# Second mixture of experts: weighted rows added into the output by indirect DMA instead of being stored, gathered and summed

## Chip, cores and metric

The kernel runs on one core of a Trainium2 chip. The metric is device time in microseconds (us) for one execution. The kernel before has a median of 2408.45 us over three runs (2401.93, 2408.45 and 2413.18).

## The reference, cut to what matters

The input is x, 4096 tokens of 256 features, and a 4096 x 4096 adjacency matrix. Two layers follow each other. Layer 0 is a graph convolution with a Mamba scan and then a mixture of eight experts; layer 1 is a graph convolution and then a mixture of six experts with three matrices each. The change touches only the last mixture:

```
rh = relu(features @ router_w1 + router_b1)          # features = layernorm(x)
expert_logits = softmax(rh @ router_w2 + router_b2)
top_w, top_i = top_k(expert_logits, 2)               # two experts of six per token
routing_weights = softmax(top_w)
h1 = relu(features @ expert_w1 + expert_b1)
h2 = relu(h1 @ expert_w2 + expert_b2)
expert_out = h2 @ expert_w3 + expert_b3
x = x + sum over the two chosen experts of routing_weights * expert_out
```

So each output row is the token's row of x (called x3 in the kernel) plus two weighted expert rows.

## The kernel before, in words

Tokens are handled in eight chunks of 512 (four groups of 128 partitions). The last mixture is split in two dispatches: `d1a` has chunks 0 to 5, `d1b` chunks 6 and 7 (lines 1452 to 1456). A `Dispatch` (L163) routes tokens to experts. Its normalised tokens go to a DRAM table `xd` (L473); a `Part` builds index tables in `tables` (L293): `src`, the row of `xd` behind each slot, and `dst`, the row of `ys` in which the slot's result belongs. An expert tile is 256 slots of one expert, in two halves j = 0 and 1 of 128. There are 27 tiles for `d1a` and 11 for `d1b` (list `few`, L1636), 38 in all, run in that order.

One tile, `tile_of` (L528): two indirect gathers on GpSimd's queue bring its rows into `xk` (`fetch`, L427 to L433, four buffers); SyncE's queue brings three matrices `wk` of 256 KB and the bias row `bk` (L535, L538); TensorE transposes (L542), VectorE copies to `xkT` (L546), TensorE runs two layers (L521) that ScalarE evacuates (L525). `finish` (L498) then multiplies by the third matrix into `ps_y` (L502), VectorE adds the bias into `yk` (L510, three buffers; in the last tile by halves, L507), and `put` (L435) sends each half by an indirect DMA from GpSimd's queue to its rows of `ys` (L437). The finish of tile k-1 is written between the first and second layers of tile k. The framework's scheduler orders each engine's list when the kernel is built; the lists run in order. Puts go to distinct rows; one put waits only for the put four before it.

The sums stand behind the tiles. `combine` (L559) reads a chunk's two result rows per token from `ys` into `yg` (L570), after the dispatch's last puts, and two VectorE operations per 128 tokens (L577) multiply by the routing weights `wv` and add x3. `to_out` (L1618) stores the chunk `oc` to the output (L1626). The six chunks of `d1a` are summed while the tiles of `d1b` run (function `also`, L1664); the two of `d1b` after the last tile, their loads shared by SyncE's and ScalarE's queues. At the very end a flag is computed; VectorE's copy `flagi` (L1689) waits for the last put, every engine loads it (L1690), and a branch (L1694) skips a rarely needed second computation.

Routing of chunks 0 to 6 is done inside the loop of the second graph convolution (`route_of`, called at step j2 of each chunk; 16 steps per chunk, TensorE line L1555); chunk 7 is routed by `routing` while the first tiles run.

Of the kernel before, what the change touches and what calls it, by code (L numbers as in the profile page):

```python
# [30 lines left out]
def kernel(ctx: ExitStack, tc: tile.TileContext, out: bass.AP, **a):  # L31
# [131 lines left out]
    class Dispatch:  # L163
# [4 lines left out]
        def __init__(self, pool, E, name, batches, c0=0):  # L168

            self.E, self.pool, self.name, self.T, self.c0 = E, pool, name, batches, c0  # L170
            self.t0 = [sum(batches[:b]) for b in range(len(batches))]
# [6 lines left out]
            self.xd = dram.tile([NT * P, D], F32, name=f"{name}_xd")  # L178

            self.S = 1 << (NT // TPC - 1).bit_length()  # L180
            self.ys = dram.tile([2 * self.S * CW + self.K * TR, D], F32, name=f"{name}_ys")
            self.count = pool.tile([P, 1, E], F32, name=f"{name}_count")
            self.start()
            self.sent = []
# [93 lines left out]
    class Part:  # L278
# [3 lines left out]
        def __init__(self, dp, name, F, c0=0, full=False, xd=None):  # L282
            self.dp, self.name, self.F, self.c0, self.full = dp, name, F, c0, full
            self.C = F * TR // P
            self.xd = dp.xd if xd is None else xd
            pool = dp.pool
            self.src = pool.tile([P, self.C], I32, name=f"{name}_src")
            self.dst = pool.tile([P, self.C], I32, name=f"{name}_dst")
            self.exps = pool.tile([P, F], I32, name=f"{name}_exps")
            self.tiles = pool.tile([1, 1], F32, name=f"{name}_tiles")  # L290
            self.used = pool.tile([P, E0], F32, name=f"{name}_used") if full else None

        def tables(self, ps, tp, biases, NG, other=None, hots=None):  # L293
# [108 lines left out]

            nc.vector.tensor_scalar(grp, grp, TPC - 1, None, ALU.bitwise_and)
# [31 lines left out]
        def put(self, k, yk, j):  # L435
            dp, c = self.dp, k * (TR // P) + j
            s_ = nc.gpsimd.indirect_dma_start(  # L437
                out=dp.ys[:, :],
                out_offset=bass.IndirectOffsetOnAxis(ap=self.dst[:, c:c + 1], axis=0),
                in_=yk[:, j, :], in_offset=None,  # L440
            )

            for o in dp.sent[-3:]:
                tc.declare_no_dep(s_.ins, o.ins, reason="distinct rows")
            if len(dp.sent) > 3:
                after(s_, dp.sent[-4])
            dp.sent.append(s_)
# [9 lines left out]
    class Route:  # L457
# [9 lines left out]
        def prepare(self, b):  # L467
# [5 lines left out]
            nc.sync.dma_start(tokens(dp.xd, b), xn)  # L473
# [17 lines left out]

    def expert_tiles(jobs, psum, pool, weights, bias_out, layers, kb_out, also=None):
# [4 lines left out]
        def finish(dp, k, w, bk, hT, parts=1):  # L497
            ps = ps_o.tile([P, 2, D], F32, name="ps_y")  # L498
            yk = pool.tile([P, 2, D], F32, name="yk", bufs=3)
            for j in range(2):  # L500
# [5 lines left out]
                if parts == 2:  # L506
                    nc.vector.tensor_tensor(yk[:, j, :], ps[:, j, :], bk, ALU.add)  # L507
                    dp.put(k, yk, j)
            if parts == 1:
# [18 lines left out]
        def tile_of(dp, k, prev):  # L528
            e = dp.expert(k)
            xk = pool.tile([P, 2, D], F32, name="xk", bufs=4)  # L530
# [15 lines left out]
            nc.vector.tensor_copy(hT, ps)  # L546
            for n, (mb, func) in enumerate(layers):
# [3 lines left out]
            return dp, k, ws[-1], bk, hT  # L551
# [817 lines left out]
    with ExitStack() as s2:  # L1369
        with ExitStack() as st:  # L1370
# [83 lines left out]
            Dispatch(keep1, E1, "d1a", [TPC] * SPLIT),  # L1454
            Dispatch(keep1, E1, "d1b", [TPC] * (NC - SPLIT), SPLIT),
# [123 lines left out]

        early = [route1(d, wk, ps_m, ("m", "m", "m"), 4) for d in dp1]  # L1580

        def route_of(c):
# [9 lines left out]
            def step(j2):  # L1592
                if j2 == 2:
# [22 lines left out]
    stores = []  # L1616

    def to_out(d, b, pool, parts=1, queue=nc.sync, bufs=3, later=False):  # L1618


        c, T = d.c0 + b, TPC // parts
        o = pool.tile([P, TPC, D], F32, name="oc")
        sent = []

        def store(part):
            sent.append(nc.sync.dma_start(tokens(out, c)[:, part, :], o[:, part, :]))  # L1626
            return sent

        rows = x3[:, c * TPC:(c + 1) * TPC, :]
        for i, _ in enumerate(combine(d, pool, b, rows, o, parts, queue, bufs)):  # L1630
            if not later:
                store(slice(i * T, (i + 1) * T))
        return (lambda: store(slice(0, TPC))) if later else sent
# [3 lines left out]
    with ExitStack() as s4:  # L1637
# [10 lines left out]
        def routing():  # L1648
# [3 lines left out]
            yield  # L1652
            yield from part1s[1].tables(
# [4 lines left out]
        ready, held, op = list(range(SPLIT)), [], []  # L1658

        def also(n):  # L1660
            if n == few[0]:
                assert next(pieces, None) is None
                sr.close()
                op.append(s4.enter_context(tc.tile_pool(name="out1", bufs=2, reuse_waits="tile")))  # L1664
            elif n < few[0]:
                if n > 2:
                    next(pieces, None)
            else:

                while held:  # L1670
                    stores.append(held.pop()())
                if (n - few[0]) % 3 != 0 and ready:
                    held.append(to_out(dp1[0], ready.pop(0), op[0], bufs=4, later=True))

        tiles1([(d, k) for d, f in zip(part1s, few) for k in range(f)], psums, tp, also)
        assert not ready and not held

        for b in range(NC - SPLIT):
            stores.append(to_out(dp1[1], b, op[0], 2 * (b + 1), nc.scalar, 4))
# [14 lines left out]
    with tc.If(again > 0):  # L1694
# [57 lines left out]
        with ExitStack() as s3:  # L1752
# [21 lines left out]
            for c in range(NC):  # L1774
                for new in to_out(d, c, op):
                    for old in stores[c]:
                        after(new, old)
# [67 lines left out]
```

## Time and profile before

| what | value |
|---|---|
| median of the runs | 2408.45 us |
| the profiled execution's own time | 2390.19 us |
| span of its profile | 2388.4 us |
| mean granted TensorE clock | 0.968 |
| TensorE matmul busy | 2232.7 us (93%) |
| VectorE, ScalarE, GpSimd busy | 1647.1, 1197.2, 1149.4 us |
| DMA on SP's and ACT's hardware queues | 54.5 and 0.2% of 16 engines' span |
| DMA on GpSimd's software queue | 19.4% |
| tiles of the last mixture, first put to last put | 2133.6 to 2369.6 us |

The span is smaller than the execution's own time by 1.8 us. A group line names the source line, the engine, the operation, output and inputs, the count, busy time, the mean duration, and the idle time just before with its releaser. DMA-issuing instructions are not counted as busy on the page, but the timeline shows them with their duration. The time to landing of a DMA counts from the start of the issuing instruction.

### The profile page before, as it was taken

To read this page: it belongs to the slowest core of one execution; us is meant where nothing else is said; L and a number is where in the kernel's file an instruction comes from. 1 tells how busy PE (TensorE), PEld (TensorE's weight loads), DVE (VectorE), ACT (ScalarE), POOL (GpSimd) and SP (SyncE) were. 2 spreads that over 40 slices of the span, in tenths; PEclk is the share of its full clock that TensorE was granted. 3 is DMA by queue.
4 is the path that set the end of the run, shared out by engine and by line. 5 is a ranking of instruction groups with operands and counts; after the bars stand their busy time and mean duration, and the time that the engine had idled before them with its cause. 6 is when DMAs were issued, how large, how long until landed. Compare 5 with 4: busy or idle time off the path is not lost. (4 is left out here: it accounts for less than half of the span.)

```text
span 2388.4 us, 28122 instructions
## 1 busy us (share of the span) xinstructions
PE 2232.7 (93%) x9010; PEld 1624.8 (68%) x9010; DVE 1647.1 (69%) x2455; ACT 1197.2 (50%) x2056; POOL 1149.4 (48%) x836
## 2 busy tenths in 40 slices
PE   8999999999999999897997999889999999999985
PEld 7665665656566655554666888667788888878874
DVE  2069999999999999999986411182666666734233
ACT  4255666575556657476753322144555555633321
POOL 1057787777877777777644555310000000046652
PEclk9999999999999999998998999989999999999998
DMA  7278899999999999998848877541444444457787
GB/s 239 82 232 229 237 276 239 270 247 270 248 252 268 234 273 237 276 266 234 280 143 276 283 235 231 164 165 61 132 142 149 144 147 142 149 167 224 245 279 238
DMA packets 295136, 513.69 MB, mean 215 GB/s; under 512 B 25648, under 2 KB 160944, under 8 KB 294080
## 3 DMA queue, kind: packets, MB, share of 16 engines
q1 hardware_dynamic: 246400, 411.07, 54.5%
q0 software_dynamic: 47424, 99.12, 19.4%
q8 instruction: 75, 1.23, 0.2%
q10 hardware_dynamic: 1152, 1.57, 0.2%
q14 instruction: 85, 0.70, 0.1%
HBM read 406.03 MB, written 44.83 MB: 189 GB/s over the span
## 5 line engine op out<-in xcount | busy, mean ns | idle before, releaser
L1146 POOL TENSOR_TENSOR db<-du,bb 128x1024 f32<-128x1024 f32 x256 | 607.0, 2371 | 314.5 <-DVE hc L1179 77.4
L1169 DVE TENSOR_TENSOR_SCAN db<-da,state,db 128x512 f32<-128x512 f32 x512 | 627.4, 1266 | 22.2 <-ACT da L1162 19.9
L675 PE MATMUL pt<-at,gn 128*128 128x256 f32 x2048 | 478.0, 386 | 14.6 <-ACT gn L87 9.3
L675 PEld LDWEIGHTS pt<-at,gn 128*128 128x128 f32 x2048 | 396.1, 194 | 135.5 <-issue 63.3
L1162 ACT ACTIVATE da<-dt,negA 128x512 f32<-128x512 f32 x512 | 346.0, 688 | 245.7 <-DVE db L1169 236.1
L1555 PE MATMUL pf<-gn,f 128*128 128x256 f32 x2048 | 452.6, 380 | 0.5 <-ACT gn L1528 0.5
L1555 PEld LDWEIGHTS pf<-gn,f 128*128 128x128 f32 x2048 | 386.5, 190 | 57.8 <-issue 6.4
L1179 DVE TENSOR_TENSOR hc<-db,cb 128x1024 f32<-128x1024 f32 x256 | 328.0, 1281 | 18.3 <-issue 0.4
L1196 PE MATMUL psy<-hc,ident 128*128 128x512 f32 x560 | 291.1, 614 | 2.4 <-DMA hc<-hc 1.4
L81 POOL TENSOR_TENSOR ln_rs<-ln_rs,mhalf 128x4 f32<-128x4 f32 (+1 forms) x25 | 32.8, 1314 | 511.0 <-DVE ln_rs L80 510.5
L510 DVE TENSOR_TENSOR yk<-ps_y,bk 128x512 f32<-128x512 f32 x71 | 49.1, 691 | 291.0 <-PE ps_y L502 262.8
L1544 ACT ACTIVATE f<-f 128x1024 f32<-128x1024 f32 x128 | 134.6, 1057 | 201.4 <-DVE f L1543 136.8
L521 PE MATMUL ps_h<-xkT,wk 128*128 128x256 f32 x864 | 213.1, 387 | 15.0 <-DVE xkT L546 10.8
L502 PE MATMUL ps_y<-wk,hk 128*128 128x256 f32 x864 | 212.7, 382 | 1.4 <-DVE yk L507 1.0
L1183 POOL DMA_DIRECT2D hc<-hc x232 | 202.0, 871 | 0.2
L521 PEld LDWEIGHTS ps_h<-xkT,wk 128*128 128x128 f32 x864 | 159.1, 192 | 49.7 <-ACT hk L525 14.6
L1543 DVE TENSOR_SCALAR f<-at 128x1024 f32<-128x1024 f32 x128 | 88.3, 690 | 149.6 <-PE pf L1555 137.0
L502 PEld LDWEIGHTS ps_y<-wk,hk 128*128 128x128 f32 x864 | 162.0, 191 | 24.5 <-ACT hk L525 1.9
L1196 PEld LDWEIGHTS psy<-hc,ident 128*128 128x128 f32 x560 | 105.0, 194 | 83.3 <-issue 58.5
L1550 DVE SCALAR_TENSOR_TENSOR cnt<-at,cnt 128x1024 bf16<-128x1024 f32 x120 | 146.1, 1217 | 17.4 <-DMA at<-in_adjT_dram 17.1
L1545 ACT ACTIVATE f<-f 128x1024 f32<-128x1024 f32 x128 | 134.5, 1055 | 3.5
L791 PE MATMUL ps_xz<-hT,w_in 128*128 128x512 f32 x256 | 117.0, 600 | 14.3 <-ACT hT L775 7.5
(329 smaller groups left out, 2530.2 us busy)
## 6 DMA issues: line engine op xcount, KB each, us to landing
at<-in_adjT_dram SPq DMA_DIRECT2D x256, 512.0 KB, 4.4
bb<-bcd SPq DMA_DIRECT2D x128, 512.0 KB, 6.0
cb<-bcd SPq DMA_DIRECT2D x128, 512.0 KB, 5.3
hc<-hc POOLq DMA_DIRECT2D x232, 256.0 KB, 6.0
wk<-in_L_ffn_W_dram SPq DMA_DIRECT2D x70, 512.0 KB, 5.4
wk<-in_L_ffn_expert_w_dram SPq DMA_DIRECT2D x114, 256.0 KB, 4.1
yg<-d_ys SPq DMA_DIRECT2D x14, 512.0 KB, 4.3
yd<-us SPq DMA_DIRECT2D x6, 1024.0 KB, 9.2
```

The lines of the kernel that those rows point to most:

```text
L502: nc.tensor.matmul(ps[:, j, :], hT[:, m, j * P:(j + 1) * P], w[:, m, :], start=(m == 0), stop=(m == kb_out - 1),)
L521: nc.tensor.matmul(ps[:, j, :], w[:, d, m * P:(m + 1) * P], xT[:, d, :], start=(d == 0), stop=(d == DB - 1),)
L675: nc.tensor.matmul(pt[:, k, :], xl[:, j, k * P:(k + 1) * P], at[:, jj, :], start=(j == 0 and k == 0), stop=(j == NT - 1 and k == DB - 1),)
L1146: nc.gpsimd.tensor_tensor(self.db, self.f.du[self.half][:, self.mi:self.mi + 1, :].to_broadcast([P, 2, CW]), self.bb, ALU.mult,)
L1162: nc.scalar.activation(da, self.f.dt[self.half][:, self.mi, :], AF.Exp, scale=negA[:, self.m, n:n + 1])
L1169: nc.vector.tensor_tensor_scan(self.db[:, j, :], da, self.db[:, j, :], state[:, self.m, n:n + 1], ALU.mult, ALU.add,)
L1179: nc.vector.tensor_tensor(self.hc, self.db, self.cb, ALU.mult)
L1183: nc.gpsimd.dma_start(self.hc[:, 0, :], self.hc[:, 1, :], accum_op=ALU.add)
L1196: nc.tensor.matmul(f.psy[m], ident, self.hc[:, j, :], start=False, stop=(self.g == GS - 1 and j == last),)
L1544: nc.scalar.activation(f, f, AF.Square)
L1550: nc.vector.scalar_tensor_tensor(cnt, at, 0.0, cnt, ALU.is_gt, ALU.add)
L1555: nc.tensor.matmul(pf[:, t, :], f[:, jj, t * P:(t + 1) * P], gn[:, j, :], start=(j == 0 and t % 2 == 0), stop=(j == NT - 1 and t % 2 == 1),)
```

## The change

`Dispatch` of the last mixture gets the kernel's output as its accumulator: `acc=out`. There is no `ys` for it, no `combine`, no `oc` and no store behind the tiles. Instead:

- `to_acc` stores each chunk's x3 rows to the output first, as the base (one store of 512 KB per chunk on SyncE's queue, at step 9 of the following chunk's loop, for the last chunk in `routing`).
- The table `xd` has 258 columns instead of 256; `weights` writes the two routing weights of each token into the last two (one more DMA per chunk on SyncE's queue), so `xk` brings them along with the row.
- A bit `sel` per slot tells which of the two weights applies; three small VectorE operations make `wt`.
- VectorE computes `yk = bk * wt` and then `yk = ps_y * wt + yk`, per half.
- `put` adds `yk` to the output's rows: an indirect DMA with add. Both halves of a tile wait for both puts of the tile before (same dispatch), and for the base stores.

```diff
+            self.acc, self.W = acc, D if acc is None else D + 2
-            self.xd = dram.tile([NT * P, D], F32, name=f"{name}_xd")
+            self.xd = dram.tile([NT * P, self.W], F32, name=f"{name}_xd")
...
         def put(self, k, yk, j):
             dp, c = self.dp, k * (TR // P) + j
+            if dp.acc is not None:
+                s_ = nc.gpsimd.indirect_dma_start(
+                    out=dp.acc[:, :],
+                    out_offset=bass.IndirectOffsetOnAxis(ap=self.dst[:, c:c + 1], axis=0),
+                    in_=yk[:, j, :], in_offset=None, bounds_check=N - 1, oob_is_err=False,
+                    compute_op=ALU.add,
+                )
+
+                for o in dp.sent[-2 - j:len(dp.sent) - j]:
+                    after(s_, o)
+                for o in dp.base:
+                    after(s_, o)
+                dp.sent.append(s_)
+                return
...
+        def weights(self, b):
+            dp = self.dp
+            t0 = dp.t0[b]
+            nc.sync.dma_start(tokens(dp.xd, b)[:, :, D:], dp.wv[:, t0:t0 + dp.T[b], :])
...
+            if wt is not None:
+                for j in range(2):
+                    nc.vector.tensor_scalar(yk[:, j, :], bk, wt[:, j:j + 1], None, ALU.mult)
...
+                if wt is not None:
+                    nc.vector.scalar_tensor_tensor(
+                        yk[:, j, :], ps[:, j, :], wt[:, j:j + 1], yk[:, j, :], ALU.mult, ALU.add
+                    )
+                    dp.put(k, yk, j)
...
+            if dp.sel is not None:
+                both = pool.tile([P, 2, 2], F32, name="wt2")
+                wt = pool.tile([P, 2], F32, name="wt")
+                sel = dp.sel[:, 2 * k:2 * k + 2]
+                for i, op in enumerate((ALU.is_le, ALU.is_gt)):
+                    nc.vector.scalar_tensor_tensor(
+                        both[:, i, :], sel, 0.5, xk[:, :, D + i], op, ALU.mult
+                    )
+                nc.vector.tensor_tensor(wt, both[:, 0, :], both[:, 1, :], ALU.add)
...
+        def to_acc(c):
+            d = dp1[c >= SPLIT]
+            d.base.append(
+                nc.sync.dma_start(tokens(out, c), x3[:, c * TPC:(c + 1) * TPC, :])
+            )
...
+                if j2 == 9:
+                    to_acc(c)
+                    d.weights(c - d.dp.c0)
...
-                while held:
-                    stores.append(held.pop()())
-                if (n - few[0]) % 3 != 0 and ready:
-                    held.append(to_out(dp1[0], ready.pop(0), op[0], bufs=4, later=True))
...
-        for b in range(NC - SPLIT):
-            stores.append(to_out(dp1[1], b, op[0], 2 * (b + 1), nc.scalar, 4))
```

Slots without a token get a `dst` beyond the last row, which the bounds check drops; `tables` ends earlier, with six operations in place of twelve behind the biases.

## Prediction

> **What bounds the kernel now.** I read the page first (TensorE is busy 93% of the span), then the sums by stage, then the timeline of the last stage, then the times to landing. Sums by stage: window, then PE, PEld, DVE, ACT, POOL busy, granted clock, DMA share, GB/s.
>
> ```profile
> 2160.00:2280.00 120.00, 119.72 (x585) 99.01 (x584) 34.13 (x78) 39.13 (x83) 79.22 (x81) 1.00 0.79 243
> 2296.00:2370.00 74.00, 61.72 (x265) 48.04 (x263) 33.07 (x69) 18.02 (x38) 31.09 (x32) 0.95 0.81 279
> 2370.00:2389.00 19.00, 0.00 (x0) 0.00 (x0) 6.74 (x17) 0.00 (x0) 0.61 (x1) 0.55 0.55 178
> ```
>
> In `d1a`'s tiles TensorE is full; in `d1b`'s, which share the DMA with the sums of `d1a`, it is not; and 19 us at the end have no matmul. The change can win only in the last two rows, and must not lose the first. GpSimd's queue in the steady part (start, duration; idle before and its releaser):
>
> ```profile
> 2284.85 1.00 POOL L437 DMA_INDIRECT d1a_ys<-yk,d1ap_dst  x1 [1.24 <-DVE yk L510]
> 2286.15 1.00 POOL L437 DMA_INDIRECT d1a_ys<-yk,d1ap_dst  x1 [0.30 <-issue]
> 2287.46 0.98 POOL L430 DMA_INDIRECT xk<-d1b_xd,d1bp_src  x1 [0.30 <-PE ps_h L521]
> 2288.74 0.96 POOL L430 DMA_INDIRECT xk<-d1b_xd,d1bp_src  x1 [0.31 <-issue]
> 2290.88 0.99 POOL L437 DMA_INDIRECT d1a_ys<-yk,d1ap_dst  x1 [1.18 <-DVE yk L510]
> ```
>
> A tile takes 2290.88 - 2284.85 = 6.03 us, TensorE's pace. The second put of a tile starts 1.30 us after the first, so it has 4.73 us until the next tile's first put. No put waits for its predecessor's landing today. How long landings take, puts from 2140 to 2290 us first:
>
> ```profile
> DMA to landing us min/median/max: 3.5/4.6/6.2
> ```
>
> and the one accumulating DMA the kernel already has, `hc<-hc` of the scan (SBUF to SBUF, 256 KB, twice a put; 600 to 800 us):
>
> ```profile
> DMA to landing us min/median/max: 3.3/6.0/8.3
> ```
>
> The end:
>
> ```profile
> 2369.64 2.41 DMA d1b_ys<-yk,d1bp_dst
> ...
> 2372.58 5.30 DMA yg<-d1b_ys
> ...
> 2381.63 0.89 DVE oc L577 x2
> ```
>
> A put with idle engines lands in 2.41 us; from there, 2372.05, to the span's end are 16.3 us of loads, sums, stores and closing.
>
> **What the Trainium skill says.** "DMA: Bandwidth & Descriptors", Rules for kernel authors: an accumulating DMA reads its destination and writes it later, and another write in between is lost, so the earlier semaphore has to be awaited; the new waits are therefore real ones. "Collectives: The Full Stack", The bandwidth ceiling: the add needs two source reads, hence two read descriptors per chunk. The trace agrees in size: in 600 to 800 us the software queue holds 36.0% of 16 engines for 48 such DMAs, 0.360 x 200 x 16 / 48 = 24.0 engine-us per 256 KB, 12.0 per 128 KB; in 2160 to 2280 us 27.2% serves 81 plain puts and gathers, 0.272 x 120 x 16 / 81 = 6.45 per 128 KB. "DMA: Bandwidth & Descriptors", How a descriptor splits into AXI transactions: a row not starting on 256 B fetches from the boundary below. By that, 1032-byte rows take an estimated 33 to 40 beats against 32; no run here shows it.
>
> **The change, part by part.**
>
> *Removed.* (1) Behind the last put: 12 loads, 16 operations of 0.48 us, 6 stores. What must stay after its landing is `flagi`, the loads and branch (SP waits 2.7 us at L1694 of the list of waits) and the closing; at least 5 us, at most today's 16.3. I take 10, so 6.3 gained. (2) The sums of `d1a`: first `d1b` put 2296.92, eleventh tile's first put 2367.99, ten intervals of 7.11 us against 6.04: 10.7 us gained if the steady pace holds. (3) 64 sums of 0.48 us on VectorE, 31 us, otherwise beside matmuls. (4) Six operations of the `dst` table: nothing, VectorE has 34.13 busy of 120 us. (5) 38 x 256 - 8192 = 1536 of 9728 slots are empty, and the bounds check drops them: up to 16% fewer bytes in the puts; 0 taken, since the fullest engine sets a landing.
>
> *Added, hidden.* VectorE per tile: L510's 0.69 us becomes two fused operations like L577 (0.48), two products (0.2 to 0.5 each, between the smallest operations and L577) and three of about 0.18 (as rt_lg's 128x24): about 2.2 in place of 0.69, some 2.9 of 6.04 with `xkT`. Uncovered it would lengthen only the last tile, by about 0.5. SyncE's queue: eight base stores of 512 KB, moved from behind the tiles into the loop with DMA share 0.49 (1900 to 2100 us; TensorE 197.65 of 200), where `at` is loaded up to four buffers ahead; uncovered, 8 x 3.4 us (the landing of today's stores) = 27. Eight `weights` stores of 8-byte pieces: no row shows one; from 0 to 4.5 us each (the median of the 64 KB `bcd` store). They wait for `wv`, three steps of 452.6/128 = 3.54 us after `choose`; for the last chunk that chain took 5.7 us (rt_lg 2149.98 to wv 2155.67), so SyncE's `at` loads are not held. For chunk 7 the `wk` loads behind may be held some us, against three weight buffers. I take 0. The wider fetch: 3 to 25% more beats, at most 1.6 engine-us, landing 4.1 now and fetched ahead into four buffers: 0. Bounds check and add in the issue: unknown; `hc`'s issue takes 0.87 us against 0.99, so a gain of 0.1 to a loss of 0.3 on each of the two issues in a tile's chain; 0 taken.
>
> *Added, on the path.* Each put waits for both puts of the tile before. It waits on GpSimd's queue, so the fetches behind wait too (three tiles ahead, harmless at first), and `yk` has three buffers, so after that VectorE, then TensorE, run at the puts' pace. That pace is P = 1.30 (first to second put) + L (landing of the second) + 0.1 (semaphore to next issue, as 2298.09 to 2298.21 on SP), or 6.04 if longer. So L decides; it hides up to 4.64, and plain puts stand at 4.6.
>
> L for an add: from below 4.6, since nothing shows an add to HBM landing sooner than a plain put under equal load; from above 4.6 x 2 = 9.2, if the doubled engine time stretches all of it. Between: 12.0 - 6.45 = 5.5 engine-us more, 0.35 us on each of 16 engines, about doubled to 0.7 as they serve other queues in turn (share 0.79), plus 0.4 for reading the destination, an estimate (gathers of as many bytes land in 4.1, so a read is not slow): 5.7. `hc` with its 6.0 for twice the bytes speaks for this order. P = 7.1. The share then is (0.79 x 96.6 + 11.1) / (16 x 7.1) = 0.77, no longer load than now.
>
> *Sum,* on the profiled execution. First put 2133.6, 37 intervals of 7.1 = 262.7, second put 1.3, landing with idle engines 3.3 (the fastest `hc`), ending 10: 2410.9, against 2388.4: +22.5 us. The profiled execution (2390.19) is 0.8% below the median; I put the difference on the median: 2408.45 + 22.5 = 2431. In general 2220 + 37 L, not below 2392 (P = 6.04: 2133.6 + 223.5 + 14.6 = 2371.7, so -16.7).
>
> **The rivals.** *The add lands as a plain put* (L up to 4.77): the chain hides, TensorE sets 6.04 and the removed sums are pure gain: 2392. For it: fast `hc` at 3.3; stores of the sums no longer compete. Against: the doubled engine time. It decides at L = 5.09, where 2220 + 37 L = 2408. *A draw* (L 4.77 to 5.42): about 2409. *Rows added one after another* (L above 7.2, up to 9.2): 2486 to 2560; speaking against: `hc` moves twice as much in 6.0. *The waits do not act as written,* the scheduler placing puts late enough: same as the first rival, 2392; against it, only 1.2 us of idle stands before a first put.
>
> **Chances.** Forecast (L 5.42 to 7.2) 0.54; hidden chain 0.20; draw 0.14; slow rows 0.12. This kernel's measurement tells about 0.5% (12 us) from no change. Slower 0.66, same 0.14, faster 0.20. The range runs from the hidden chain with a tail 4 us shorter, 2388, to L = 7.2, 2486; 0.12 lies above. The forecast case alone has 2421 to 2486.
>
> **What would show it.** In the trace after: an idle time before first puts released by "DMA out", growing from 1.2 us; put landings near 5.7; tile intervals near 7.1 with TensorE at some 85% in 2160 to 2280; no `yg` and `oc`; about 15 us from last put to the end. I am wrong if landings stay under 5.1, if put issues grow past 1.3, or if L1555's stage lengthens.

## The result, and the profile after

| kernel | median, us | runs |
|---|---|---|
| before | 2409.74 | 2401.93 to 2413.18 (4) |
| after | 2547.68 | 2543.72 to 2549.4 (4) |

The change makes the kernel slower: ratio 1.0575, interval 1.0546 to 1.0604. The forecast had the sign but not the size: 2431.0, with a range to 2486. The profiled execution of after took 2546.7 us, with a span of 2544.8.

Here is the part of the span in which the change lies, read from the puts in both traces (start of the issuing instruction on GpSimd's queue; "tile" is the mean interval from one tile's first put to the next's):

| | before | after |
|---|---|---|
| first put, us | 2133.6 | 2132.8 |
| tile, all 37 intervals, us | 6.34 | 10.55 |
| first to second put of a tile, median, us | 1.29 | 4.64 |
| issue of one put, median, us | 0.99 | 1.57 |
| last put, us | 2369.6 | 2527.8 |
| last put to the end of the span, us | 18.8 | 17.0 |

The start is the same to 0.8 us and the end differs by 1.8 us. The whole loss lies in the tile interval: 37 x (10.55 - 6.34) = 156 us, which is the difference of the spans (2544.8 - 2388.4 = 156.4). The medians differ by 138 us only, since the profiled execution of before (2390.19 us) was some 20 us faster than its median. First the sums by stage of after, with the columns of the prediction (window, PE, PEld, DVE, ACT, POOL, clock, DMA share, GB/s):

```profile
2160.00:2280.00 120.00, 80.21 (x322) 62.20 (x321) 37.43 (x159) 21.27 (x46) 56.86 (x44) 0.83 0.57 135
2350.00:2400.00 50.00, 31.94 (x128) 24.95 (x128) 11.69 (x39) 8.06 (x17) 23.11 (x18) 0.88 0.62 142
2528.00:2545.00 17.00, 0.00 (x0) 0.00 (x0) 0.14 (x1) 0.00 (x0) 1.36 (x1) 0.50 0.08 12
```

TensorE was full in the first window before (119.72 of 120 us) and is now busy for 80.21. No engine has taken its place: VectorE has 37 of 120 us, GpSimd 57, and the DMA share fell from 0.79 to 0.57. VectorE alone has slightly more work than before (34.13). If nothing is near full, the stage waits on a latency, not on a throughput. GpSimd's queue shows which (start, duration; idle before and its releaser):

```profile
2288.56 1.62 POOL L458 DMA_INDIRECT out_dram<-yk,d1ap_dst  x1 [2.57 <-DVE yk L541]
2293.15 1.57 POOL L458 DMA_INDIRECT out_dram<-yk,d1ap_dst  x1 [2.98 <-issue]
2295.03 1.01 POOL L450 DMA_INDIRECT xk<-d1a_xd,d1ap_src  x1 [0.30 <-PE ps_y L544]
2296.34 1.00 POOL L450 DMA_INDIRECT xk<-d1a_xd,d1ap_src  x1 [0.30 <-issue]
2297.73 1.62 POOL L458 DMA_INDIRECT out_dram<-yk,d1ap_dst  x1 [0.39 <-DVE yk L541]
2299.65 0.97 POOL L450 DMA_INDIRECT xk<-d1a_xd,d1ap_src  x1 [0.30 <-PE ps_h L568]
2303.17 1.58 POOL L458 DMA_INDIRECT out_dram<-yk,d1ap_dst  x1 [2.55 <-DVE wt L603]
```

Before, the second put of a tile followed the first at 1.30 us. Here they stand at 2288.56 and 2293.15, 4.59 us apart, and again at 2297.73 and 2303.17. The page calls the idle time "issue"; in the order of instructions the second put waits on the semaphore of the first put's DMA, and the trace has that wait ending at 2292.40, 3.84 us after the first put started. In the second pair the same wait ends at 2302.41, 4.68 us after the first put started; VectorE's `wt`, which the page names, comes at 2302.87 and costs little more. So the second half of a tile is not sent before the first has landed. The chain of waits shows the bare links at the end, where no fetch is left on the queue (start, duration, what):

```profile
2510.64 3.87 DMA out_dram<-yk,d1bp_dst
2514.50 0.02 issue
2514.53 0.02 POOLq L458
2514.54 0.49 issue
2515.03 0.03 POOLq L458
2515.06 0.20 issue
2515.26 3.76 DMA out_dram<-yk,d1bp_dst
...
2527.79 3.70 DMA out_dram<-yk,d1bp_dst
2531.50 0.02 issue
2531.52 0.14 DVE flagi L1733
```

One link is 2515.26 - 2510.64 = 4.62 us: 3.87 of landing, then 0.75 from the semaphore to the next issue. There are 75 such links for 76 puts; on the mean one takes 395.0 / 75 = 5.27 us, since fetches and waits for VectorE stand between some of them. How it reaches TensorE stands in the list of waits from 2160 to 2330 us (who waits, for whom: us in total, times, longest):

```profile
DVE yk L541 <- DMA out_dram<-yk,d1ap_dst: 81.9, 15, 12.1
PEld ps_h L568 <- DVE xkT L593: 39.7, 7, 11.6
...
PE ps_h L568 <- DVE xkT L593: 36.8, 7, 11.2
```

VectorE's multiplication `yk = bk * wt` waits for a `yk` buffer, that is, for a landed put; the copy to `xkT` stands behind it on VectorE's list; TensorE waits for `xkT`.

The pages have the groups of TensorE's first layer, before and after, and of the puts (count, busy, mean ns, then idle before and its releasers):

```profile
L521 PE MATMUL ps_h<-xkT,wk 128*128 128x256 f32 x864 | 213.1, 387 | 15.0 <-DVE xkT L546 10.8
...
L568 PE MATMUL ps_h<-xkT,wk 128*128 128x256 f32 x864 | 236.3, 418 | 99.9 <-DVE xkT L593 95.2
...
L458 POOL DMA_INDIRECT out_dram<-yk,d1ap_dst x54 | 85.9, 1591 | 140.1 <-issue 66.6
```

The wait for `xkT` before the matmuls of this layer grew from 10.8 to 95.2 us. That is the largest part of what the change costs.

### The profile page after: what moved, and what is told of

Its sections match the earlier page's. It is cut to its first block, busy times and chain, and to the rows that moved or that the text cites. A ratio compares the mean times of both kernels' runs of the same rounds, so it can differ in the third digit from the quotient of the medians.

```text
span 2544.8 us, 28318 instructions
## 1 busy us (share of the span) xinstructions
PE 2272.5 (89%) x9010; PEld 1646.7 (65%) x9010; DVE 1660.8 (65%) x2606; ACT 1196.7 (47%) x2056; POOL 1196.3 (47%) x836
## 5 line engine op out<-in xcount | busy, mean ns | idle before, releaser
L568 PE MATMUL ps_h<-xkT,wk 128*128 128x256 f32 x864 | 236.3, 418 | 99.9 <-DVE xkT L593 95.2
L568 PEld LDWEIGHTS ps_h<-xkT,wk 128*128 128x128 f32 x864 | 172.4, 209 | 144.2 <-DVE xkT L593 103.9
L544 PE MATMUL ps_y<-wk,hk 128*128 128x256 f32 x864 | 229.5, 403 | 18.7 <-DVE yk L549 16.4
L1601 ACT ACTIVATE f<-f 128x1024 f32<-128x1024 f32 x128 | 134.6, 1057 | 197.9 <-DVE f L1600 131.4
L544 PEld LDWEIGHTS ps_y<-wk,hk 128*128 128x128 f32 x864 | 170.7, 204 | 49.0 <-DVE yk L549 19.2
L572 ACT ACTIVATE hk<-ps_h,d1ap_b 128x256 f32<-128x256 f32 x108 | 51.0, 473 | 225.2 <-PE ps_h L568 207.5
L458 POOL DMA_INDIRECT out_dram<-yk,d1ap_dst x54 | 85.9, 1591 | 140.1 <-issue 66.6
L557 DVE TENSOR_TENSOR yk<-ps_y,bk 128x512 f32<-128x512 f32 x34 | 23.5, 691 | 176.0 <-PE ps_y L544 174.0
```

What stands on the lines that cost most here:

```text
L544: nc.tensor.matmul(ps[:, j, :], hT[:, m, j * P:(j + 1) * P], w[:, m, :], start=(m == 0), stop=(m == kb_out - 1),)
L568: nc.tensor.matmul(ps[:, j, :], w[:, d, m * P:(m + 1) * P], xT[:, d, :], start=(d == 0), stop=(d == DB - 1),)
L1601: nc.scalar.activation(f, f, AF.Square)
```

## The experiments

They were run in six groups (e1 to e4, e5 to e8, e9 to e11, e12, e13 to e15, e16 to e18); each ratio is to runs of the kernel before in the same group. The level of the kernel before moved from group to group: 2391.11, 2408.36, 2394.67, 2392.73, 2406.76 and 2392.41 us. That of chain-bound kernels hardly moved (after 2547.68, its variants e11 and e15 2550.66 and 2548.04 in groups at different levels). So ratios of different groups are not compared where they differ by less than 0.7%.

**Theory.** The time is that of a chain of landings with 75 links, not 37, since the two halves of a tile also wait for each other. **Rivals.** The add itself is slow (in the queue, or in the DMA engines); the bounds check or the longer issue on GpSimd's queue is; the buffers between VectorE and the puts are too few.

**e1_halves_free.** The second half of a tile is declared independent of the first; the waits for the tile before stay.

```diff
+                if j == 1:
+                    tc.declare_no_dep(s_.ins, dp.sent[-1].ins, reason="distinct rows")
```

> The changed kernel, with the two adding puts of one tile declared independent (their rows are distinct); every other wait stays. Theory A (the time went into a wait nobody wrote: the framework orders any two writes to the output, so the second half of a tile waits for the first, 75 links in the chain instead of 37): the second put of a tile starts 1.9 us after the first instead of 4.6, a tile takes 1.9 + about 4.2 + 0.75 = 6.8 to 7.3 us instead of 10.5, and the span falls from 2545 to 2404 to 2422 us, 0.7 to 1.5% above the kernel before. Theory B (the add itself is slow, in its issue or in the DMA engines, and waits only show it): the two adds of a tile still take about 9 us and the span stays above 2500 us.

Measured: 2448.24 us, ratio 1.023 (1.0212 to 1.0248). Three lines of GpSimd's queue, and the times to landing of its puts:

```profile
2251.48 1.62 POOL L458 DMA_INDIRECT out_dram<-yk,d1ap_dst  x1 [0.60 <-DVE yk L543]
2253.40 1.56 POOL L458 DMA_INDIRECT out_dram<-yk,d1ap_dst  x1 [0.31 <-issue]
...
2258.78 1.62 POOL L458 DMA_INDIRECT out_dram<-yk,d1ap_dst  x1 [1.21 <-DVE yk L543]
```

```profile
DMA to landing us min/median/max: 2.7/4.7/7.3
```

Removing 38 of the links takes 98 us off the span (2544.8 to 2446.8), so they were the greater part of the loss. Theory A had the span lower still, at 2404 to 2422, and a tile at 6.8 to 7.3 us. What is left is exactly the structure that the prediction priced at 7.1 us a tile; it measures 7.93: 1.92 from first to second put, 4.70 mean landing of the second, 1.31 from there to the next tile's first put.

**e2_no_add** writes in place of adding, with all waits kept; it leaves out the sum of the rows.

```diff
-                    compute_op=ALU.add,
```

> The changed kernel with a plain write in place of the add, all waits and the bounds check kept; the sum of the two experts and of the base is left out, so later writes replace earlier ones. Theory A: the chain of 75 links stays and only the link is shorter: 75 x (3.0 to 3.6 + 0.7) = 280 to 320 us, span 2430 to 2470 us; if the 1.58 us of issue belongs to the add it falls to about 1.0 and the lower end holds, if it belongs to the bounds check it stays. Theory B: without the add a put costs what it did, and the span falls to 2390 us or less.

Measured: 2471.76 us, ratio 1.0331 (1.0314 to 1.0349). The puts of the first dispatch (ns minimum, median, maximum) and all landings:

```profile
L458 POOL DMA_INDIRECT out_dram<-yk,d1ap_dst x54: 967/1000/1050, 2134.0 to 2373.1; - x54
...
DMA to landing us min/median/max: 2.1/3.1/6.5
```

Without the add a landing takes 3.1 us in the middle and an issue 1.00, and the kernel is still 3.3% slower than before; its span of 2471.1 us is at the upper end of theory A. So about half of the loss stands without any add (83 of 156 us of span); the add makes each link longer by about 0.95 us (mean tile 8.65 against 10.55 us, two links in a tile).

**e3_before_in_turn** is the reverse: the kernel before, with its puts of the last mixture no longer declared independent.

```diff
-            for o in dp.sent[-3:]:
+            for o in dp.sent[-3:] if dp.E != E1 else []:
```

> The kernel before, with the puts of the second mixture no longer declared independent, so that each waits for the one before; nothing is added into the output. Theory A: the wait alone costs most of the loss: a put lands in about 3.3 us when alone, a link is 3.7 to 4.0 us, a tile 7.4 to 8 us in place of 6.04, span 2430 to 2465 us (1.8 to 3.2% above the kernel before). Theory B: plain puts take turns at little cost, under 1%.

Measured: 2480.13 us, ratio 1.036 (1.034 to 1.038). In its trace, who waited for the puts of the first dispatch, and the landings (of these puts and of the twelve loads of their sums):

```profile
  POOL d1a_ys L437: 77.6, 34
...
DMA to landing us min/median/max: 2.4/3.8/8.6
```

One missing declaration, on plain writes, with the sums still in place, costs 3.6%: tiles at 8.66 us and 4.25 us between halves, more than theory A's 7.4 to 8. This is the strongest single proof of the theory, since nothing else of the change is in it.

**e4_before_bounds** gives the puts of the kernel before the bounds check.

```diff
+                 **(dict(bounds_check=2 * dp.S * CW + dp.K * TR - 1, oob_is_err=False)
+                    if dp.E == E1 else {}),
```

> The kernel before, with a bounds check on the puts of the second mixture (every index is inside, so nothing is dropped). If the bounds check makes the longer issue: an issue takes 1.58 us instead of 0.99, GpSimd's queue needs 2 x 1.9 + 2 x 1.28 = 6.3 us per tile against 6.04 of TensorE, and the span grows by 10 to 15 us (0.4 to 0.6%). If the add makes it: issues stay at 0.99 us and the time does not move.

Measured: 2393.42 us, ratio 1.0007 (0.9995 to 1.0018). The issue stays where it was:

```profile
L437 POOL DMA_INDIRECT d1a_ys<-yk,d1ap_dst x54: 977/1007/1020, 2133.9 to 2292.7; - x54
```

The bounds check costs next to nothing, in the issue (1.01 us against 0.99) and in the time. The longer issue of after (1.57 us) must be the add's.

**e5_before_adds** lets the puts of the kernel before add, each to its own row of `ys`, which is set to zero earlier.

```diff
+                 **(dict(compute_op=ALU.add) if dp.E == E1 else {}),
```

> The kernel before, with its puts turned into adds onto rows of its own result table that are set to zero during the graph convolution (82 small stores on SyncE's queue); every row still gets one put, so no put waits for another beyond what it did. It is the add alone. Theory C (after the waits, the longer issue is the next bound: 1.57 us in place of 0.99 makes GpSimd's queue 2 x 1.88 + 2 x 1.29 = 6.3 us per tile against 6.04 of TensorE): tiles 6.3 to 6.5 us apart in the d1a part, 8 to 14 us more, 0.3 to 0.7% slower. Theory B (the add loads the DMA engines until landings hold everything up): d1a tiles 7 us or more apart, over 1.5% slower.

Measured: 2411.03 us, ratio 1.0009 (1.0001 to 1.0017). The puts, and the sums from 2160 to 2280 us:

```profile
L437 POOL DMA_INDIRECT d1a_ys<-yk,d1ap_dst x54: 1552/1584/1648, 2135.9 to 2306.0; - x54
```

```profile
2160.00:2280.00 120.00, 116.76 (x565) 95.50 (x564) 34.76 (x88) 37.30 (x80) 96.58 (x75) 1.00 0.93 230
```

The add alone costs 0.1% here, though it shows everywhere: issues at 1.58 us, GpSimd's queue busy for 96.58 of 120 us in place of 79.22, DMA share 0.93 in place of 0.79 (that trace is from a group at the lower level). GpSimd's queue is in fact full: 96.58 us and 75 gaps of 0.30 us make 119 of 120 us. The tiles of the first dispatch are 6.47 us apart, as in theory C, though the time grew by less than its 0.3 to 0.7%. In a group at the lower level the ratio might come out up to 0.7% higher (not tried), still far from 5.8%. The rival "the add is slow" falls as the cause of the loss: what is slow is waiting for it.

**e6_two_targets** adds odd tiles to a second tensor, so that a put waits only for the puts two tiles back, with the halves free. The final sum of the second tensor is left out, so odd tiles are missing in the output.

```diff
+                    out=(dp.acc if k % 2 == 0 else twin)[:, :],
...
+                keep = [o for o in dp.sent if o not in dp.of[1 - k % 2]]
+                if j == 1:
+                    tc.declare_no_dep(s_.ins, keep[-1].ins, reason="distinct rows")
+                for o in keep[-2 - j:len(keep) - j]:
```

> The changed kernel with the halves of a tile independent, and even tiles adding into the output, odd tiles into a second tensor with the same base; the sum of the two tensors is left out, so the output lacks the odd tiles. The chain then has a tile's time to spare: 1.9 + 4.7 + 0.8 = 7.4 us per two tiles. Theory C: GpSimd's queue sets 6.3 to 6.5 us per tile, span 2134 + 37 x 6.4 + 19 = 2390 us, that is no gain on the kernel before even with the final sum left out. If instead turn-taking was all, 6.04 us per tile and 2376 us.

Measured: 2408.76 us, ratio 1.0000 (0.9988 to 1.0012); tiles at 6.95 us, GpSimd's instructions busy for 88.12 of 120 us. One tile more between a put and its wait takes away another 35 us of span (2446.8 to 2411.6). The tiles do not come down to theory C's 6.3 to 6.5 us, and the removed sums still buy nothing; e9 shows a limit that takes the place of the chain.

**e7_interleaved** is a complete kernel: halves free, the two dispatches free of each other (their tokens are different), 14 tiles of the first in a row and then tiles of the two in turn.

```diff
+                mine = dp.sent[-1:] if j == 1 else []
+                for o in mine + [o for d in dp1 if d is not dp for o in d.sent + d.base]:
+                    tc.declare_no_dep(s_.ins, o.ins, reason="distinct rows")
...
+        first = 14
+        a_, b_ = jobs[:few[0]], jobs[few[0]:]
+        jobs = a_[:first]
+        for i in range(max(len(a_) - first, len(b_))):
+            jobs += b_[i:i + 1] + a_[first + i:first + i + 1]
```

> The changed kernel with the halves of a tile independent, puts of the two dispatches independent (their tokens are distinct), and the tiles of d1b set between those of d1a from the 15th tile on, so that a put waits for one two tiles back there. Complete in its result. Expected from e1 (8.3 us per tile for the first 14) and theory C (6.4 to 6.6 for the other 23): 2134 + 116 + 150 + 19 = 2419 us, about 1.1% above the kernel before; if turn-taking between tiles were not the cause of e1's remainder, it stays at e1's 2447.

Measured: 2407.94 us, ratio 0.9998 (0.9987 to 1.0008). In the part where the dispatches alternate:

```profile
2280.00:2380.00 100.00, 95.28 (x442) 75.14 (x441) 38.95 (x124) 29.84 (x63) 76.03 (x58) 1.00 0.83 208
```

Here TensorE is back at 95.28 of 100 us. The first 14 tiles still take 7.83 us each, the next 18, in turn, 6.56. It ends earlier than the 2419 us expected. So, beside the kernel before of this group, the whole loss of the change is undone by order and declarations alone, but no gain appears.

**e8_free_no_add** is e1 with plain writes; it leaves out the sum.

```diff
-                    compute_op=ALU.add,
+                if j == 1:
+                    tc.declare_no_dep(s_.ins, dp.sent[-1].ins, reason="distinct rows")
```

> The changed kernel with the halves of a tile independent and a plain write in place of the add; the sum of base and experts is left out. It leaves only the waiting of a tile for the one before: 1.3 + 3.8 to 4.3 + 0.75 = 5.9 to 6.4 us, near TensorE's 6.04. Span 2134 + 37 x 6.3 + 15 = 2382 us, from 2375 to 2400: about the kernel before. If waiting between tiles costs more than its landing, 2420 us.

Measured: 2413.27 us, ratio 1.0029 (1.0017 to 1.004), with a span of 2410.5 us, above the 2375 to 2400 expected. Repeated in another group as e16, it has 0.9995. With e1 and e2 this closes a square. In it are the spans (us) of the profiled executions, that of e16 for the last corner, since e1 and e2 are from a group at the same level:

| span, us | halves wait for each other | halves free |
|---|---|---|
| add | 2544.8 (after) | 2446.8 (e1) |
| plain write | 2471.1 (e2) | 2387.2 (e16) |

The halves' wait costs 98 us with the add and 84 without; the add costs 74 and 60 as long as puts of the tile before are waited for, some 3.4 us of it behind the last put. Both lengthen the same chain.

**e9_alternating** goes on from e7: the first dispatch is cut to five chunks, ten tiles in a row and the rest in turn, and chunk 7's base store is freed too.

```diff
-SPLIT = 6
+SPLIT = 5
...
+        first = 10
...
+            s_ = nc.sync.dma_start(tokens(out, c), x3[:, c * TPC:(c + 1) * TPC, :])
+            for o in [o for e in dp1 if e is not d for o in e.sent]:
+                tc.declare_no_dep(s_.ins, o.ins, reason="distinct rows")
```

> The changed kernel with the two halves of a tile free of each other, the first dispatch cut to five chunks (SPLIT = 5), puts of the two dispatches and chunk 7's base store free of each other, ten tiles of the first dispatch in a row and after that tiles of the two dispatches in turn. A put then waits only for a put two tiles back for most of the mixture. Theory (what costs is the chain of landings): ten tiles at 7.7 to 8.3 us, then 28 at 6.4 to 6.5 us, GpSimd's queue setting that pace (two adds of 1.57 us, two fetches of 1.0 us, three gaps); first put 2133, last put near 2390 or a little sooner, about 13 us behind it: 0.2 to 0.6% below the kernel before, ratio 0.994 to 0.998. Rival (adding as such costs, whatever the order): tile intervals stay at 7 us or more in the alternating part, ratio 1.00 to 1.01.

Measured: 2407.18 us, ratio 1.0061 (1.0047 to 1.0075). The puts came as the theory had them: nine intervals of 8.08 us, then 28 of 6.49, the last put at 2387.6. The ratio missed it, for two reasons: I had set this sum against the level of the group before (2408), where here it is 2394.67; and the end took 16.4 us, not 13 (see "The end" below). GpSimd's queue in the alternating part:

```profile
2320.10 1.62 POOL L458 DMA_INDIRECT out_dram<-yk,d1bp_dst  x1 [0.30 <-issue]
2322.03 1.58 POOL L458 DMA_INDIRECT out_dram<-yk,d1bp_dst  x1 [0.30 <-issue]
2323.91 1.56 POOL L458 DMA_INDIRECT out_dram<-yk,d1ap_dst  x1 [0.30 <-issue]
2325.78 1.56 POOL L458 DMA_INDIRECT out_dram<-yk,d1ap_dst  x1 [0.31 <-issue]
2327.64 1.02 POOL L450 DMA_INDIRECT xk<-d1a_xd,d1ap_src  x1 [0.30 <-issue]
2328.97 0.99 POOL L450 DMA_INDIRECT xk<-d1a_xd,d1ap_src  x1 [0.30 <-issue]
```

The only idle time here is the 0.30 us between two issues: the queue is full in this stretch, and from 2280 to 2380 us it is so for 92% (74.73 us and 57 gaps of 0.30 in 100 us). Its tile is 2 x (1.57 + 0.30) + 2 x (1.00 + 0.30) = 6.34 us, more than TensorE's 6.03. So where the chain is loosened, the issue of the adds is the next limit, and it stands above the pace of the kernel before.

**e10_before_again** is the kernel before, once more, for a trace from e9's group.

> The kernel before, unchanged, so that its trace on this chip stands beside the others: one look, within 0.3% of the run of the kernel before beside it. First put near 2133.6, tiles at 6.04 us in the steady part and 7.1 us beside the sums, if the first profile is typical.

Measured: 2391.05 us, span 2389.2; first put 2132.7, 6.05 us a tile in the first dispatch and 7.27 in the second, 18.8 us behind the last put. The first profile was typical.

**e11_deeper_yk** is the changed kernel with six `yk` buffers.

```diff
-            yk = pool.tile([P, 2, D], F32, name="yk", bufs=3)
+            yk = pool.tile([P, 2, D], F32, name="yk", bufs=6)
```

> The changed kernel with six yk buffers in place of three. Theory (the chain of 75 landings limits the rate, VectorE's wait for yk is only where it shows): the puts come no sooner, the tile interval stays near 10.5 us, and only TensorE runs ahead by three more tiles; time within 0.5% of the changed kernel, ratio 1.053 to 1.06 of the kernel before. Rival (the three yk buffers make the stall, since VectorE, and TensorE behind it, wait for landed puts): with twice the buffers the tile interval falls below 9 us and the time below 2490 us, ratio below 1.035.

Measured: 2550.66 us (after: 2547.68), ratio 1.0652 (1.0629 to 1.0675), a little above the theory's 1.06 since the kernel before stood lower in this group (2394.67). Tiles at 10.56 us, as in after. From 2160 to 2330 us VectorE now waits elsewhere:

```profile
DVE wt L600 <- DMA xk<-d1a_xd,d1ap_src: 65.4, 10, 10.9
```

The wait for `yk` has gone and the wait for `xk` has come: the fetches stand behind the waiting puts on GpSimd's queue. The buffers only choose where the chain shows. The rival falls.

**e12_loads_ahead** is e8 with four buffers instead of three for each expert matrix and the bias row; it leaves out the sum as e8 does.

```diff
-                w = pool.tile(shape, F32, name=f"wk{n}", bufs=3)
+                w = pool.tile(shape, F32, name=f"wk{n}", bufs=4)
...
-            bk = pool.tile([P, D], F32, name="bk", bufs=3)
+            bk = pool.tile([P, D], F32, name="bk", bufs=4)
```

> Like e8_free_no_add (halves free, plain writes in place of adds, which leaves out the sum), with four buffers instead of three for each expert matrix and its bias row, so that SyncE's loads can run one tile further ahead. In e8_free_no_add tiles take 7.09 us although nothing but the wait for the tile before is left, and TensorE sometimes waits up to 3.4 us for a matrix whose load was issued late. Theory A (the loads are held for want of buffers, and that makes the irregular stalls): tiles of the first dispatch fall from 7.36 to about 6.4 us, and the ratio to the kernel before from 1.003 to 0.99 or less. Theory B (the stalls come from the wait for the tile before, and late loads only follow from it): tile interval stays at 7.0 to 7.2 us, ratio 1.00 to 1.006.

Measured: 2389.74 us, ratio 0.9990 (0.9981 to 0.9998); tiles at 6.43 us on the mean against 7.09 in e8. The interval fell nearly as theory A has it, the ratio by only 0.4%, and the group was another one. The same edit was then put into three kernels (in e14 only for the third matrix and the bias row, since the buffers of the sums leave no more room), and at last e8 and e12 were run side by side.

**e13_interleaved_loads_ahead**, on e7:

> e7_interleaved (halves free, 14 tiles of the first dispatch in a row, then the two dispatches in turn) with four buffers instead of three for each expert matrix and the bias row. If late loads add to the stalls of its first 14 tiles (7.7 us each) as they did in e8_free_no_add: these fall to about 7.2 us, the ratio from 1.000 to 0.995 or 0.998. If its first tiles are held by the wait for the tile before (1.9 + 4 to 5 + 1.3 us) alone: ratio 0.999 to 1.001. If GpSimd's queue (6.34 us a tile) is the bound everywhere: no change.

Measured: 2411.02 us, ratio 1.0021 (1.0012 to 1.003). No gain. Its windows:

```profile
2200.00:2280.00 80.00, 66.28 (x299) 52.15 (x297) 26.40 (x85) 19.98 (x44) 56.51 (x45) 0.96 0.81 195
2280.00:2380.00 100.00, 94.12 (x440) 74.73 (x439) 39.89 (x125) 29.88 (x63) 76.60 (x58) 1.00 0.82 202
```

TensorE has 83% of the first (its first half is one dispatch alone, each tile waiting for the one before) and 94% of the second (in turn), much as in e7. The first 14 tiles take 8.0 us each, e1's pace of 7.93: that is the chain and not the loads.

**e14_before_loads_ahead**, on the kernel before:

> The kernel before with four buffers for the third matrix and the bias row (its memory has no room for a fourth of all three beside the buffers of its sums). TensorE is full in its steady part, so I expect no change there, and beside the sums at most some us: ratio 0.997 to 1.000. If it gains as much as e8_free_no_add did (20 us, 0.8%): late loads have nothing to do with the change.

Measured: 2401.53 us, ratio 0.9974 (0.9963 to 0.9986): 0.26%, less than what I count as a difference, and with nothing of the change in it.

**e15_after_loads_ahead**, on the changed kernel:

> The changed kernel with four buffers for each matrix and the bias row. Theory (75 landings in a chain set the rate): tile interval stays near 10.5 us, time 2535 to 2555 us. Rival (want of buffers is a second cause of its own): the interval falls by some 0.5 us or more, time 2530 us or less.

Measured: 2548.04 us, ratio 1.059 (1.0566 to 1.0614); tiles at 10.32 us. The chain sets the rate whatever the buffers are.

**e16_free_no_add_again, e17_loads_ahead_again, e18_before_third**: e8, e12 and the kernel before in one group. The first two leave out the sum.

> e8_free_no_add once more (halves free, plain writes; it leaves out the sum). If the stalls in it were the group's: its tile interval moves with the level of the kernel before, near 6.5 us if that is near 2392 us, near 7.1 us if it is near 2408 us. If want of buffers made them: 7.0 to 7.2 us in any group.

> e12_loads_ahead once more (four buffers for each matrix and the bias row; it leaves out the sum). If the buffers matter: at least 15 us faster than e16_free_no_add_again beside it, tile interval 6.4 us. If the group made the difference: within 5 us of e16_free_no_add_again.

> The kernel before, unchanged, for its trace in this group: within 0.3% of the runs beside it. Where the level is near 2392 us TensorE is full from 2160 to 2280 us (119.7 of 120); where it is near 2408 us I expect 113 to 117 of 120, with waits for the matrices.

Measured: e16 2391.37 us, ratio 0.9995 (0.9985 to 1.0004), tiles at 6.50 us; e17 2389.93 us, 0.9988 (0.9981 to 0.9994), tiles at 6.43 us; e18 2387.12 us, with TensorE full. Side by side the buffers give 1.4 us. The 7.09 us of e8 were the group's, not the kernel's. The window from 2160 to 2280 us of e14, from a group at the higher level, and of e18, from one at the lower:

```profile
2160.00:2280.00 120.00, 113.26 (x536) 91.44 (x536) 32.85 (x83) 35.18 (x76) 70.83 (x73) 0.99 0.71 221
```

```profile
2160.00:2280.00 120.00, 119.75 (x583) 99.14 (x582) 32.03 (x71) 39.53 (x84) 79.97 (x82) 1.00 0.80 243
```

In the first, TensorE misses some 6.5 us in 120 that it has in the second, with deeper buffers at that. Theory A of e12 falls, and with it the thought that want of buffers is a second cause.

## Why the prediction was wrong, by its own steps

**The step that failed** is "Each put waits for both puts of the tile before", with "P = 1.30 (first to second put) + L + 0.1". It let the second half of a tile start 1.30 us after the first, as in the kernel before, and counted 37 links. The kernel has 75. The framework orders two writes to the same tensor unless they are declared independent; the kernel before has such a declaration right behind its put, and the new branch returns ahead of it. The explicit waits in the diff were read as the whole list of waits; they are only what was added to it. e1 puts a price on this step: 98 us of span, of the 134 by which the span exceeds the predicted 2410.9. The rival in the prediction that came near this ("the waits do not act as written") thought of weaker waits only, never of more of them. The same holds for the sentence ahead of the prediction that both halves wait for the tile before: the second half waits for the first as well.

**The remaining 36 us** are sizes in a mechanism that e1 shows to be right. Its tile is 7.93 us against 7.1:

| term | predicted, us | measured in e1, us |
|---|---|---|
| first to second put | 1.30 | 1.92 |
| L, landing of the second put | 5.7 | 4.70 |
| landing to the next tile's first put | 0.1 | 1.31 |

- *First to second put:* the issue of an add takes 1.57 us. `hc`'s 0.87 us, from which a loss of at most 0.3 was derived, was no guide; e4 and e5 lay it on the add, not on the bounds check. A put issue past 1.3 us was one of the prediction's signs of being wrong, and it came.
- *L* was too high (landings under 5.1 us were another such sign). The heavier add is there. The Trainium skill ("Collectives: The Full Stack", The bandwidth ceiling) states two source reads for the add of a ReduceScatter; no run here shows how many reads an indirect add makes, but in e5 the DMAs of GpSimd's queue from 2160 to 2280 us, half adds and half gathers, hold 0.446 x 120 x 16 / 74 = 11.6 engine-us each, against 6.45 before. If the gathers stayed at 6.45, an add takes some 16.7, an estimate, and so more than the 12.0 taken from `hc`. The load was forecast right: e1's DMA share from 2160 to 2280 us is 0.76, against 0.77. What was too high is the base. Plain puts with the same waits (e16) land in 3.8 us, the mean of the 27 second halves whose landing the trace has, and not in 4.6; the add brings 0.9 to that, where 1.1 was expected. Why plain puts land sooner there is open.
- *0.1 us from semaphore to issue* came from SP's queue. On GpSimd's it is 0.75 us (2514.51, where the first landing of the chain above ends, to 2515.26), and in e1 up to three fetches of 1.3 us each stand between.
- *Sum:* 37 x 0.83 = 30.6 us, the first put 0.9 later and the second put's 0.6, and the end 3.8 longer, give 35.9; 2446.8 - 2410.9 = 35.9.

That the sign came right is in part luck. With the measured L of 4.70 the prediction's own 2220 + 37 L gives 2394 us, less than the kernel before: the terms at 1.30 and 0.1, and the links it did not count, made the kernel slower.

**The end.** I expected 13.3 us behind the last put's start and it is 17.0 in after. Loads, sums and stores are gone, and only 1.8 us came of it: the landing (3.70) ends at 2531.50, and 13.3 us follow for the flag, its loads, the branch and the closing. Before, 16.3 us followed the landing, but much of the closing lay beside the sums. The trace has it in GpSimd's last two long instructions, an increment of semaphores and a drain: before, they took 1.30 and 4.64 us and ran from 2377.20 to 2383.17, while VectorE summed; in after they take 1.75 and 6.40 and run from 2535.80 to 2543.97, with no other engine at work. So the "10" was the term that failed, at 13.3. "A stage removed" is not "its time removed" when something else ran beside it. Some 2 us of it come with the adds: the pair takes 8.1 to 8.2 us in all nine traces whose puts add, and 5.9 in the eleven others. Why is not shown. e7 and e9 agree: in e7, whose last tiles are of the first dispatch, `flagi` waits only for the second dispatch's last put and runs at 2375.6 us, ahead of the last put, and the end is 13.3 us; in e9 it runs at 2390.3, behind the last landing, and the end is 16.4.

**The gain of the removed sums** (10.7 us) needs the steady pace to hold to the end. It doesn't, even with the chain gone: GpSimd's queue with adds needs 6.34 us a tile (e9) against TensorE's 6.03, 37 x 0.31 = 11.5 us over the whole mixture, an estimate, and about what the sums gave. e9 beside e10 agrees: its last 28 intervals take 181.8 us, those of the kernel before 178.9. The rest of what e9 loses lies in its first nine intervals, still in the chain: 72.7 us against 57.1. The same two, the queue and the tiles left in the chain, can account for e7, which also ends at the time of the kernel before and not 0.7% below it as in the rival "hidden chain". For e6, where a put waits only for tiles two back, the queue is only argued: its 88.12 us and 70 gaps of 0.30 make 109 of 120 us.

**What held.** L and the waits decide, not bandwidth; `yk` hands the stall to VectorE and then to TensorE, which is at 67% of the first window in place of the 85% forecast; fetches wait behind the puts. "Extras on VectorE: 0" held (37.43 of 120 us busy). "SP's queue: 0" held nearly: chunk 7's base store waits 9.0 us for adding puts, once. The skill's rule that an add has to await the one before it ("DMA: Bandwidth & Descriptors", Rules for kernel authors) concerns tiles that share tokens; no run here adds to shared rows without the wait. What the wait costs, the trace shows: 4.6 us for a bare link.

**Open.** Why the level of a full TensorE stage differs by 0.7% between groups was not found; one and the same chip gave 2394.67 us in e9's group and 2406.76 in e13's. A version with fewer issues on GpSimd's queue wasn't tried.

## What to carry to other kernels

Before pricing a wait, list every wait that the new instruction has, the ones that the framework adds among them: an old instruction's declaration of independence doesn't pass to the code that takes its place. Here a read-modify-write on a shared target turned puts from a throughput cost into a chain whose price is the number of links times (landing + the way from the semaphore to the next issue), so count the links first and size L second. And when a stage goes, look for what ran beside it: here the closing and the next fullest queue took back what the sums gave.

## What was not expected of the hardware

- An indirect put with add takes GpSimd 1.57 us to issue against 0.99 to 1.00 for a plain one of the same 128 rows of 1 KB; the bounds check adds 0.02 at most (e4: 1.01, e2: 1.00).
- Between a landed DMA's semaphore and the next issue on GpSimd's queue lie about 0.75 us at the end of after, where the queue waited for it (0.78 to 0.84 in most links of e1), and 0.30 between two issues that wait for nothing.
- At the end of the mixture, where the chain is bare, the last five adds of after land in 3.87, 3.76, 2.72, 3.79 and 3.70 us, the last five plain puts of e2 in 2.41, 2.36, 2.11, 2.41 and 2.33. Some 0.6 us of the difference is the longer issue.
- GpSimd's closing (semaphores and drain) takes 8.15 us in after, whose puts add, and 5.95 in e2, whose puts do not.
- TensorE's granted clock fell to 0.83 in the starved stage (1.00 before in the same window). In it, from 2286 to 2325 us, the two groups of four matmuls of 128x256 just behind a stall of 2.2 to 5.6 us take 1.8 to 2.1 us each, and groups further on 1.03, so that such a stall costs more than its length.
